# Attention's slot in a new order, and more filler in its last group: a macaron block (MoE, attention, MoE)

## The chip, the cores and the metric

The kernel runs on one core of a Trainium2 chip. The metric is device time in microseconds (us) of one execution. The core's engines are named as in the profile: PE is TensorE (PEld its weight loads), DVE is VectorE, ACT is ScalarE, POOL is GpSimd, SP is SyncE, which here only issues DMAs. Each engine works off its own queue in order.

## The reference

The input is X, 16 x 256 tokens of width 256, in float32. A feed-forward layer, an attention layer and the same feed-forward layer again are added to it:

```python
x = x + 0.5 * ffn(layernorm(x))
x = x + attn(layernorm(x))
x = x + 0.5 * ffn(layernorm(x))
```

Attention has 16 query heads and 8 key and value heads of width 32, rotary positions, a soft cap (scores are 50 tanh(scores/50)), a causal mask and softmax. The feed-forward layer normalizes its input (RMS), and returns input plus routed experts plus a shared expert:

```python
probs = softmax(x @ w_router)              # 32 experts, the best 4 of each token
g, u = buf @ w_gate[e], buf @ w_up[e]      # up to 128 tokens per expert, hidden width 176
y = (silu(g) * u) @ w_down[e]              # scattered back with the routing weight
sh = sigmoid(x @ w_shared_gate) * ((silu(x @ sw_gate) * (x @ sw_up)) @ sw_down)   # hidden width 704
return inp + out + sh
```

## The kernel before

The 4096 tokens are 32 tiles of 128, and 4 tiles make a group `g` (`NG` = 8 groups, two sequences of 256 tokens each). The residual `x` stays on chip for the whole program. There are three stages: feed-forward 0, attention, feed-forward 1.

In a feed-forward stage, each group is routed (`route`, L227: moments, transposes `pt` to `xnT`, router product `pl`, the best four, and a store of the normalized rows to the DRAM table `xtab`). Then `slots` (L310 on) gives each expert its list of tokens. The 32 experts follow (`expert`, L408): rows are gathered from `xtab` by an indirect DMA, go through gate, up and down products, and POOL scatter-adds them into the DRAM accumulator `acc`. After all experts the sums are read back (`read_sums`, L457) and added to `x`.

The shared expert depends on no expert. It is cut into pieces and used as *filler* for PE (`shared`, L371, and `Fill`, L611). For one group the pieces are: five gate chunks (`pg`, L388, eight matmuls each), one half chunk (four matmuls), and four tiles of the down product (`po`, L400, twelve matmuls each). Each piece gives a planned cost. `Fill.take(us)` adds to a balance and emits pieces until the balance is used up; overshoot is carried on, and the balance is dropped only where no group is ready:

```python
yield 1.7 * len(at)        # a gate chunk: 3.4, the half chunk 1.7
...
yield 2.6                  # one tile of the down product
```

`fill` is the shared expert of feed-forward 0, `fill2` that of feed-forward 1. A group of `fill2` is ready (`fill2.ready`) once the next routing is far enough. What is left of `fill2` after the last expert is emitted at the end by `fill2.finish(NG)`. There, groups that are done before it (`begun`) get their sums from `add_sums` on POOL; tiles that end later go through `end`, on DVE for those the last filler finishes.

Attention works by units (g, b, m): a group, one of its two sequences, and one half of the heads; 32 units in all. `scores` (L537) is a generator with two steps. Its first step makes the products of the queries with the first 128 keys into two `big` PSUM tiles `sc`, and ACT's tanh (L556) and exp (L559) and POOL's causal select (L561) on 1024 columns each; its second step does the same for the last 128 keys, with 512 columns each. `values` (L568) multiplies the probabilities by ones and by `v` into `den` and `y`, and DVE divides. `project_out` (L595) makes the output product `poa` and adds it to `x`, once per pair of units. `project` (L467) is the preparation of a group: reading the sums of feed-forward 0, adding them, moments, the normalized rows `a`, their transposes `hT`, then eight pieces of queries, keys and values (`pq`, `pv`), where rotary positions cost DVE two and POOL two instructions per `pq` piece.

A slot `k` (the loop at L742, k = 0 to 33, with j = k mod 4 and g = k // 4) puts together work of several units and groups: scores of unit k, values of unit k-1, output projection of unit k-2, projection pieces for group g+1 (`mine`) and earlier steps for g+2 (`ahead`), routing for the last stage (`routing`), and filler (`spare_time(SPARE[j])`). In the last group and the two slots behind it there is no `mine`. In this stage the order of PE, DVE, ACT and POOL is the order in which the code is written (`manual_schedule`); outside it that holds for PE, and for POOL among the experts.

PSUM is shared by three kinds of tiles, two buffers each: `big` (scores' `sc` and the filler's `pg`), `mm` (`pq`, `pv`, `pt`, `pta`, `pl`, `po`, `poa`) and `aux` (`den`, `y`).

Of the kernel before, what the change touches and what calls it, by code (L numbers as in the profile page):

```python
# [9 lines left out]
F32 = mybir.dt.float32  # L10
# [8 lines left out]
P = 128  # L19
NB, T, C = 16, 256, 256  # L20
# [25 lines left out]
MASK_FILL, ROW_FILL = 4.0, 3.2  # L46
WARM = (16, 3)
AHEAD = 3
SPARE = (1.0, 0.0, 3.0, 4.0)
PROJECT_PIECES = ((2, 1), (0, 2), (2, 1), (0, 0))  # L50

# [41 lines left out]
def macaron_kernel(ctx: ExitStack, tc: tile.TileContext, X, Wq, Wk, Wv, Wo, w_norm, w_router, w_gate, w_up,  # L93
# [314 lines left out]
    def expert(pool, n, e, idx, wd):  # L408

        xg = pool.tile([P, XW], F32, name="xg", bufs=AHEAD + 3)  # L410
        nc.gpsimd.indirect_dma_start(  # L411
# [53 lines left out]
    made = [[] for _ in range(NG)]  # L465
# [71 lines left out]
    def scores(pool, u, qT, kT):  # L537

        _, b, m = u
        t0 = b * T
        made = []
        for k0, w in ((0, T), (P, P)):
            dst = pool.tile([P, 4, 2, w], F32, name=f"p{w}", bufs=2)
            sc = [big.tile([P, 2, 2 * T], F32, tag="big", name="sc") for _ in range(2)]
            for i in range(4):
                r = slice(HD * i, HD * (i + 1))
                nc.tensor.matmul(  # L549
                    sc[i // 2][:, i % 2, 0 : 2 * w].rearrange("p (s t) -> p s t", s=2),  # L550
                    lhsT=kT[r, m, t0 + k0 : t0 + k0 + P], rhs=qT[r, m, :, t0 + T - w : t0 + T],
                    start=True, stop=True,
                )
            parts = [dst[:, 2 * h : 2 * h + 2].rearrange("p j s t -> p j (s t)") for h in range(2)]
            for h in range(2):
                nc.scalar.activation(parts[h], sc[h][:, :, 0 : 2 * w], AF.Tanh, scale=QK_SCALE / SOFTCAP)  # L556
            for h in range(2):

                nc.scalar.activation(parts[h], parts[h], AF.Exp, scale=SOFTCAP)  # L559
                diag = dst[:, 2 * h : 2 * h + 2, :, 0:P].rearrange("p j s t -> p (j s) t")  # L560
                nc.gpsimd.affine_select(  # L561
                    out=diag, in_=diag, compare_op=ALU.is_ge, fill=0.0,
                    base=0, pattern=[[0, 4], [1, P]], channel_multiplier=-1,
                )
            made.append(dst)
            yield made

    def values(pool, u, v, pa, pb, yT):  # L568


        _, b, m = u
        y = ps1.tile([P, 2, T], F32, tag="aux", name="y")
        den = ps1.tile([P, 2, T], F32, tag="aux", name="den")
        for late in range(2):
            for dst in (den, y):
                for i in range(4):
                    r = slice(HD * i, HD * (i + 1))
                    w = ones if dst is den else v[:, 2 * b + late, 4 * m + i, :]
                    if late:
                        nc.tensor.matmul(dst[r, :, P:T], lhsT=w, rhs=pb[:, i], start=False, stop=True)  # L580
                    else:
                        nc.tensor.matmul(dst[r], lhsT=w, rhs=pa[:, i], start=True, stop=False)  # L582

        dT = pool.tile([P, 2 * T // HD, HD], F32, name="dT")
        nc.vector.transpose(dT.rearrange("p n d -> p (n d)"), den.rearrange("p s t -> p (s t)"))
        rc = stat.tile([P, 2 * T // HD, 1], F32, name="rc")
        nc.vector.reciprocal(rc, dT[:, :, 0:1])
        rb = pool.tile([P, 2 * T // HD, HD], F32, name="rb")
        nc.vector.transpose(rb, rc.to_broadcast([P, 2 * T // HD, HD]))
        nc.vector.tensor_mul(  # L590
            yT[:, m].rearrange("p s t -> p (s t)"), y.rearrange("p s t -> p (s t)"),
            rb.rearrange("p n d -> p (n d)"),
        )

    def project_out(g, b, yT):  # L595
        for qh in range(2):
            t = g * GT + 2 * b + qh
            po = ps1.tile([P, C], F32, tag="mm", name="poa")
            for c in range(4):
                nc.tensor.matmul(  # L600
                    po, lhsT=yT[:, c // 2, c % 2, qh * P : (qh + 1) * P], rhs=wo[:, c // 2, c % 2, :],
                    start=(c == 0), stop=(c == 3),
                )
            nc.vector.tensor_add(x[:, t, :], po, x[:, t, :])


    def advance(work, count=1):
        for _ in range(count if work else 0):
            next(work, None)
# [32 lines left out]
    def feed_forward(n, pool, works, fill):  # L642
# [34 lines left out]

        for e in range(AHEAD):
            next(steps[e])
        with tc.manual_schedule(engines={ET.Pool}):  # L680
            for e in range(E + 2):
                if e + AHEAD < E:
                    next(steps[e + AHEAD])
                for late in range(3):
# [50 lines left out]
    units = [(g, b, m) for g in range(NG) for b in range(2) for m in range(2)]  # L735
    with tc.tile_pool(name="attn", bufs=1, reuse_waits="tile") as pool:
        probs, outs, routing = {}, {}, {}

        def spare_time(us):
            (fill if fill.done < NG else fill2).take(us)  # L740

        for k in range(len(units) + 2):  # L742
            g, j = divmod(k, 4)
            u = units[k] if k < len(units) else None
            mine, ahead = projects.get(g + 1), projects.get(g + 2)

            def unit_values():
                if 1 <= k <= len(units):
                    d = units[k - 1]
                    if d[2] == 0:  # L750
                        outs[d[:2]] = pool.tile([P, 2, 2, T], F32, name="yT")
                    values(pool, d, made[d[0]][2], *probs.pop(d), outs[d[:2]])

            if u:
                parts = scores(pool, u, *made[g][:2])
                next(parts)
            if k >= 2 and units[k - 2][2] == 1:
                d = units[k - 2][:2]  # L760
                project_out(*d, outs.pop(d))
            advance(mine, PROJECT_PIECES[j][0])
            if mine is None and j % 2 == 0:
                unit_values()
            if u:
                probs[u] = next(parts)

            if j == 0:
                advance(routing.get(g - 2))
            if j == 2:  # L770
                advance(routing.get(g - 2))
            if j == 3:
                advance(ahead)
            if mine is not None or j % 2:
                unit_values()


            if j == 3:
                advance(routing.get(g - 1))
            spare_time(SPARE[j])  # L780
            advance(mine, PROJECT_PIECES[j][1])
            if j == 1 and g >= 1:
                routing[g - 1] = route(1, g - 1)
                next(routing[g - 1])
                advance(routing.get(g - 2))
                fill2.ready = max(g - 1, 0)
            if j == 2:
                advance(routing.get(g - 1))
                advance(routing.get(g - 2))
            if j == 0:  # L790
                advance(routing.get(g - 2))

            fill.finish(min(g + 3, NG))
            if j == 3:
                advance(ahead, 2)
            elif j < 2:
                advance(ahead)
            if j == 3 and g + 3 < NG:
                projects[g + 3] = project(pp, g + 3)
                next(projects[g + 3])  # L800
        advance(routing[NG - 2], 2)
        advance(routing[NG - 1])
        fill2.ready = NG - 1
        fill2.take(LAST_FILL)
        ordered.close()
# [39 lines left out]
```

## Time and profile before

| | |
|---|---|
| median of 3 runs | 1089.79 us (1088.53 to 1090.43) |
| the profiled execution: time, and span of its instructions | 1091.85 us, 1090.1 us |
| granted TensorE clock, mean | 0.992 |
| busy share: PE, DVE, POOL, ACT | 96%, 54%, 45%, 37% |
| chain that ended last, by engine | PE 84%, DVE 8%, POOL 3%, ACT 2% |
| first scores of unit 0 begin | 395.3 us |
| last values of attention begin | 788.67 us |
| last scatter-add of an expert begins | 1057.43 us |

The profile shows one execution: the busy time of each engine, what each instruction waited for, the clock that was granted to TensorE, and the DMA traffic. In the timeline a line gives the start, the length, the engine, the source line and the operation, the tiles written and read, and how many instructions were merged. A bracket gives the idle time just before, and what ended it. In the table by windows a row gives the stretch and its length, then the busy time of PE, PEld, DVE, ACT and POOL, and last the granted clock, the DMA share and GB/s.

### The profile page before, as it was taken

What the parts mean: (1) busy time and instruction counts of PE and PEld (TensorE: products, weight loads), DVE (VectorE), ACT (ScalarE), POOL (GpSimd) and SP (SyncE); (2) the same over time, 40 slices, a digit from 0 to 9 for tenths busy, and PEclk for the clock granted to TensorE, in tenths of its full rate; (3) what the DMA queues carried; (4) which work ended last, traced back from release to release, by engine and by line L of the source; (5) the groups of instructions that cost most, each with busy time, mean ns of one, the idle gap of its engine ahead of it and who ended that gap; (6) DMA issues with size and microseconds to landing.
All of it is one profiled execution on the core that took longest, in us unless ns stands there. A gap on an engine that the chain in (4) does not pass through costs nothing.

```text
span 1090.1 us, 15694 instructions
## 1 busy us (share of the span) xinstructions
PE 1049.8 (96%) x5446; PEld 655.0 (60%) x5446; DVE 587.5 (54%) x1653; ACT 400.4 (37%) x761; POOL 492.3 (45%) x600
## 2 busy tenths in 40 slices
PE   9899999999999999989999999999999999999998
PEld 6656556777767544445455555454466467768675
DVE  5756655444453445656565657573656644444443
ACT  3333111222221256574647474745621112222211
POOL 4600102455552297777475656551411024555536
PEclk9999999999999999999999999998999999999999
DMA  8721611677773000000101010000030017777839
GB/s 268 211 96 66 202 37 37 150 168 165 171 166 57 33 21 20 1 20 2 41 1 41 2 41 1 23 17 6 23 82 22 1 33 155 161 171 155 175 60 308
DMA packets 137871, 93.00 MB, mean 85 GB/s; under 512 B 80512, under 2 KB 135104, under 8 KB 137792
## 3 DMA queue, kind: packets, MB, share of 16 engines
q1 hardware_dynamic: 125504, 74.16, 24.4%
q0 software_dynamic: 12288, 17.83, 9.4%
q8 instruction: 44, 0.72, 0.3%
q14 instruction: 35, 0.29, 0.1%
HBM read 60.99 MB, written 30.97 MB: 84 GB/s over the span
## 4 chain that ended last, share of the span: by engine, by line
PE 84%; DVE 8%; POOL 3%; ACT 2%; issue 2%; DMA 1%; SPq 0%; POOLq 0%; DVEq 0%; ACTq 0%
PE pg L388 26%; PE po L400 14%; PE pge L435 8%; PE pq L500 7%; PE poe L448 5%; PE poa L600 5%; PE sc L549 5%; PE pv L528 3%; PE den L582 2%; PE y L582 2%; PE pl L274 2%; PE pte L427 1%; DVE act L394 1%; DVE act L393 1%; DVE xr L246 1%
## 5 line engine op out<-in xcount | busy, mean ns | idle before, releaser
L388 PE MATMUL pg<-xnT,sw 128*128 128x512 f32 x704 | 320.0, 599 | 2.5 <-ACT p L556 1.8
L388 PEld LDWEIGHTS pg<-xnT,sw 128*128 128x128 f32 x704 | 130.4, 191 | 139.4 <-issue 130.4
L400 PE MATMUL po<-swd,act 128*128 128x256 f32 x768 | 182.9, 388 | 10.6 <-DVE act L394 6.4
L451 POOL DMA_INDIRECT acc<-y,idx x64 | 101.4, 1584 | 181.5 <-DMA acc<-y,idx 69.9
L400 PEld LDWEIGHTS po<-swd,act 128*128 128x128 f32 x768 | 144.8, 193 | 40.7 <-issue 12.1
L393 DVE SCALAR_TENSOR_TENSOR act<-act,pg 128x512 f32<-128x512 f32 x96 | 65.6, 684 | 172.6 <-ACT act L392 125.7
L392 ACT ACTIVATE act<-pg 128x512 f32<-128x512 f32 x96 | 57.3, 597 | 274.6 <-PE pg L388 266.8
L556 ACT ACTIVATE p<-sc 128x512 f32<-128x512 f32 (+1 forms) x128 | 97.5, 809 | 112.7 <-PE sc L549 109.1
L561 POOL TENSOR_SCALAR_AFFINE_SELECT p<-p 128x512 f32<-128x512 f32 x128 | 78.9, 640 | 84.8 <-ACT p L559 73.0
L411 POOL DMA_INDIRECT xg<-xtab,idx x64 | 67.9, 1062 | 78.8 <-DVE idx L366 59.9
L435 PE MATMUL pge<-xgT,wgu 128*112 128x128 f32 (+1 forms) x768 | 95.7, 274 | 5.8 <-issue 4.4
L559 ACT ACTIVATE p<-p 128x512 f32<-128x512 f32 (+1 forms) x128 | 100.9, 844 | 0.0
L435 PEld LDWEIGHTS pge<-xgT,wgu 128*112 128x112 f32 (+1 forms) x768 | 88.8, 182 | 8.6 <-issue 8.5
L549 PE MATMUL sc<-qT,kT 32*128 32x256 f32 (+1 forms) x512 | 68.6, 535 | 4.7 <-DVE act L394 3.4
L404 DVE SCALAR_TENSOR_TENSOR x<-po,sg,x 128x256 f32<-128x256 f32 x64 | 30.8, 482 | 78.1 <-PE po L400 74.4
L508 POOL TENSOR_TENSOR qs<-qs,kc 128x512 f32<-128x512 f32 x48 | 61.4, 1278 | 13.4 <-DVE qs L503 13.4
L394 DVE TENSOR_TENSOR act<-act,pg 128x512 f32<-128x512 f32 x96 | 65.7, 684 | 2.4
L430 ACT ACTIVATE xgT<-pte,wnorm 128x128 f32<-128x128 f32 x128 | 40.0, 365 | 71.3 <-PE pte L427 68.7
L448 PE MATMUL poe<-wd,sie 112*128 112x256 f32 x256 | 65.9, 379 | 0.1
L600 PE MATMUL poa<-wo,yT 128*128 128x256 f32 x256 | 61.5, 394 | 1.7 <-DVE qT L507 1.6
L500 PE MATMUL pq<-hT,wq 128*128 128x512 f32 x128 | 60.9, 599 | 0.0
L600 PEld LDWEIGHTS poa<-wo,yT 128*128 128x128 f32 x256 | 48.4, 194 | 20.0 <-issue 4.6
(116 smaller groups left out, 1317.7 us busy)
## 6 DMA issues: line engine op xcount, KB each, us to landing
xtab<-xr SPq DMA_DIRECT2D x16, 576.0 KB
acc<-zero SPq DMA_DIRECT2D x2, 4224.0 KB
a<-acc SPq DMA_DIRECT2D x16, 512.0 KB
wgu<-in_L_ffn_w_gate SPq DMA_DIRECT2D x64, 112.0 KB
wgu<-in_L_ffn_w_up SPq DMA_DIRECT2D x64, 112.0 KB
wd<-in_L_ffn_w_down SPq DMA_DIRECT2D x64, 112.0 KB
wgu<-in_L_ffn_w_gate SPq DMA_DIRECT2D x64, 64.0 KB
wgu<-in_L_ffn_w_up SPq DMA_DIRECT2D x64, 64.0 KB
```

Source lines behind the costliest of these rows:

```text
L388: nc.tensor.matmul(pg[:, s, :], lhsT=sw[:, c, w0 : w0 + P], rhs=xnT[:, c, cols], start=(c == 0), stop=(c == 1))
L394: nc.vector.tensor_mul(si, si, b)
L400: nc.tensor.matmul(po, lhsT=act[:, k, t * P : (t + 1) * P], rhs=swd[:, k, :], start=(k == 0), stop=(k == len(FC) - 1),)
L435: nc.tensor.matmul(pg[:fw, n_, :], lhsT=wgu[:, c, w0 : w0 + fw], rhs=xgT[:, c, :], start=(c == 0), stop=(c == 1))
L448: nc.tensor.matmul(po, lhsT=si[:, k, :], rhs=wd[:, k, :], start=(k == 0), stop=(k == 1))
L451: nc.gpsimd.indirect_dma_start(out=acc[n], out_offset=bass.IndirectOffsetOnAxis(ap=idx[:, e : e + 1], axis=0), in_=y, in_offset=None, boun ...
L500: nc.tensor.matmul(pq, lhsT=weights[:, c, :], rhs=hT[:, c, :], start=(c == 0), stop=(c == 1))
L549: nc.tensor.matmul(sc[i // 2][:, i % 2, 0 : 2 * w].rearrange("p (s t) -> p s t", s=2), lhsT=kT[r, m, t0 + k0 : t0 + k0 + P], rhs=qT[r, m, ...
L556: nc.scalar.activation(parts[h], sc[h][:, :, 0 : 2 * w], AF.Tanh, scale=QK_SCALE / SOFTCAP)
L559: nc.scalar.activation(parts[h], parts[h], AF.Exp, scale=SOFTCAP)
L561: nc.gpsimd.affine_select(out=diag, in_=diag, compare_op=ALU.is_ge, fill=0.0, base=0, pattern=[[0, 4], [1, P]], channel_multiplier=-1,)
L600: nc.tensor.matmul(po, lhsT=yT[:, c // 2, c % 2, qh * P : (qh + 1) * P], rhs=wo[:, c // 2, c % 2, :], start=(c == 0), stop=(c == 3),)
```

## The change

First scores are taken a slot earlier: those of unit k+1 are emitted in slot k. A slot now runs second scores of its unit, then values of unit k-1, then first scores of unit k+1, and only then routing, `ahead`, output projection, projection pieces and filler. The separate order for the last group (values ahead of second scores in even slots) goes. Each slot without `mine` (k = 28 to 33) asks for 3.0 more of filler. One step of the routing of group g-2 moves from the end of slot j = 2 to behind the filler of slot j = 3.

```diff
+LAST_SPARE = 3.0
 SPARE = (1.0, 0.0, 3.0, 4.0)
 PROJECT_PIECES = ((2, 1), (0, 2), (2, 1), (0, 0))
...
+        def first_scores(u):
+            parts[u] = scores(pool, u, *made[u[0]][:2])
+            next(parts[u])
+
+        parts = {}
+        first_scores(units[0])
         for k in range(len(units) + 2):
             g, j = divmod(k, 4)
             u = units[k] if k < len(units) else None
             mine, ahead = projects.get(g + 1), projects.get(g + 2)
 
-            def unit_values():
-                if 1 <= k <= len(units):
-                    d = units[k - 1]
-                    if d[2] == 0:
-                        outs[d[:2]] = pool.tile([P, 2, 2, T], F32, name="yT")
-                    values(pool, d, made[d[0]][2], *probs.pop(d), outs[d[:2]])
...
             if u:
-                parts = scores(pool, u, *made[g][:2])
-                next(parts)
+                probs[u] = next(parts[u])
+            if 1 <= k <= len(units):
+                d = units[k - 1]
+                if d[2] == 0:
+                    outs[d[:2]] = pool.tile([P, 2, 2, T], F32, name="yT")
+                values(pool, d, made[d[0]][2], *probs.pop(d), outs[d[:2]])
+            if k + 1 < len(units):
+                first_scores(units[k + 1])
+
+            if j == 0 or j == 2:
+                advance(routing.get(g - 2))
+            if j == 3:
+                advance(ahead)
             if k >= 2 and units[k - 2][2] == 1:
                 d = units[k - 2][:2]
                 project_out(*d, outs.pop(d))
             advance(mine, PROJECT_PIECES[j][0])
-            if mine is None and j % 2 == 0:
-                unit_values()
-            if u:
-                probs[u] = next(parts)
-
-            if j == 0:
-                advance(routing.get(g - 2))
-            if j == 2:
-                advance(routing.get(g - 2))
-            if j == 3:
-                advance(ahead)
-            if mine is not None or j % 2:
-                unit_values()
...
             if j == 3:
                 advance(routing.get(g - 1))
-            spare_time(SPARE[j])
+            spare_time(SPARE[j] + (0.0 if mine else LAST_SPARE))
+            if j == 3:
+                advance(routing.get(g - 2))
             advance(mine, PROJECT_PIECES[j][1])
...
             if j == 2:
                 advance(routing.get(g - 1))
-                advance(routing.get(g - 2))
```

## The prediction

> **What bounds the kernel now.** I read the page first: its totals, then its slices.
>
> ```profile
> span 1090.1 us, 15694 instructions
> PE 1049.8 (96%) x5446; PEld 655.0 (60%) x5446; DVE 587.5 (54%) x1653; ACT 400.4 (37%) x761; POOL 492.3 (45%) x600
> DMA  8721611677773000000101010000030017777839
> ```
>
> TensorE (PE) is busy 96% of the span; only some 40 us are idle. A change that removes no PE instruction can gain no more than idle time and throttled clock. In the DMA row the attention stage (slices 15 to 30) moves almost nothing, while the last slice is full. So the two ends of this change lie in places with different limits: attention on PE, the end of the program perhaps on DMA.
>
> Next the timeline of PE, attention's last group, where no projection work is left to hide waits:
>
> ```profile
> 740.30 1.13 PE L549 MATMUL sc<-qT,kT 32*128 32x512 f32 x4
> 742.50 1.65 PE L549 MATMUL sc<-qT,kT 32*128 32x512 f32 x4 [1.07 <-DVE act L394]
> ...
> 749.37 3.70 PE L388 MATMUL pg<-xnT,sw 128*128 128x512 f32 x8 [0.74 <-ACT p L556]
> ```
>
> A bracket is PE's idle time and its releaser. Both waits are for the two `big` PSUM buffers, which scores and the filler's gate products share. Six such waits from 740 to 810 us (1.07, 0.74, 0.64, 1.10, 1.07, 1.52) make 6.1 us. Then the table by windows, whose third-last number is the granted clock:
>
> ```profile
> 742.00:744.00 2.00, 1.50 (x4) 0.30 (x4) 0.45 (x1) 0.56 (x1) 0.00 (x0) 0.74 0.00 0
> 744.00:746.00 2.00, 2.00 (x14) 0.59 (x16) 0.00 (x0) 1.81 (x2) 0.00 (x0) 0.50 0.04 8
> 756.00:758.00 2.00, 2.00 (x7) 1.44 (x6) 0.00 (x0) 1.62 (x2) 0.00 (x0) 0.66 0.00 0
> 758.00:760.00 2.00, 2.00 (x7) 1.53 (x6) 0.25 (x1) 1.29 (x2) 1.27 (x2) 0.50 0.00 0
> ```
>
> Twice the clock fell to half. With 0.90 at 746 and 0.99 at 760 the lost time is 2 x (0.26 + 0.50 + 0.10 + 0.34 + 0.50 + 0.01) = 3.4 us. Last, the end of the program: the chain in order of time, then windows.
>
> ```profile
> 1056.98 18.88 PE pg L388 x44
> 1075.86 2.16 PE po L400 x10
> ```
> ```profile
> 1063.00:1065.00 2.00, 2.00 (x6) 0.80 (x6) 0.49 (x1) 0.60 (x1) 0.00 (x0) 1.00 1.00 352
> 1073.00:1075.00 2.00, 2.00 (x6) 0.92 (x5) 0.19 (x1) 0.60 (x1) 2.00 (x2) 1.00 1.09 349
> 1083.00:1085.00 2.00, 2.00 (x11) 1.77 (x10) 0.91 (x2) 0.00 (x0) 0.00 (x0) 1.00 1.08 374
> ```
>
> The last scatter-add of an expert starts at 1057.43. From there the chain is PE filler, but beside it DMA is also full (shares of 1.00 to 1.09) from 1063 to 1085: it reads 8 x 512 KB of sums and writes 4.19 MB of output. PE and DMA end within some 3 us of each other. This row decides my forecast.
>
> **The filler is moved, not removed.** `Fill.take` is a ledger: a piece costs 3.4 (gate chunk), 1.7 (half chunk) or 2.6 (a tile's down product); a group costs 5 x 3.4 + 1.7 + 4 x 2.6 = 29.1, all eight 232.8. Before, demands on `fill2` are 48 in attention, 8 LAST_FILL, then 9 + 4 + 46 + 6 + 81.6 in the last feed-forward: 202.6. Seven groups are 203.7, so one whole group is left, which is what the end of the chain shows: 44 gate matmuls, then 48 down ones. With LAST_SPARE six slots (k = 28 to 33) ask 3.0 more each. Six groups are ready then, so nothing is dropped: demand 220.6, and 12.1 is left (a half chunk and four down products). Piece by piece, slots 28 to 33 with LAST_FILL take 35.9 instead of 18.9: five more chunks. A chunk is eight matmuls of 128x512; at the end of the program the tanhs of successive chunks start at 1063.88, 1067.32 and 1070.75, a pitch of 3.43 us. That gives **+17.1 us of PE in attention**, and the PE work after the last scatter falls from 29.5 us (1056.98 to 1086.53) to 12.4.
>
> **What the last group takes up.** At most the 6.1 us idle and 3.4 us clock: 9.5. But the new order makes waits of its own. Slot 28 now runs two chunks straight before the second scores of unit 29. The second chunk's buffer comes free after ACT 0.60, DVE 0.69 and 0.69, about 2.1 us; a `pt` pair (0.6) and one score tile (0.3) cover 0.9, leaving 1.2. A chunk right behind first scores waits for their tanh (1.02 us for 1024 columns) at 0.4 to 0.5, twice; a down product behind a half chunk queues behind exp (1.06 each) at 0.6. That is about 3 us, and I leave 1 us of clock. Taken up: 5.5, bounds 0 and 9.5.
>
> **A rule that speaks against it.** The row is a half clock after single gaps of 1.07 and 0.64 us. The Trainium skill ("TensorE: Matmul & The Clock Gate", section "HAM oscillation — how this bites in real kernels") says it takes PE-idle gaps above about 3.4 us to bring the clock down; by it no wait here would cost clock, the filler could only buy idle time, and the forecast below would rise by the 2.4 us of clock I credit. The row shows the clock lost at smaller gaps, so I go by the row.
>
> **The start.** First scores of unit 0 now stand directly before its second scores. The tanh pair took 396.47 to 398.41, exp to 400.30; the second half's tanh needs 1.09 more, so first scores of unit 1 come near 401 and PE idles some 4 us where two projection pieces ran before. But unit 1 then starts 1.5 us earlier than before (402.56) and the old waits in its slot (1.11 and 0.21 at 405) go. Through the two `v` pieces I reach 415.7 where before was at 413.8: **+1.9**, bounds 0 and 4.4.
>
> **The middle, 28 slots.** Nothing is added. Before, idle PE from 412.72 to 727.73 is 2.97 + 0.20 + 0.20 + 0.54 + 1.23 = 5.1 us. In the new order second scores find tanh done a slot ago. First scores of the next unit wait for both second-half tanhs (1.09), and the values between (about 2.7) cover that; without them it would be 1.5 a slot. Moved with first scores: ACT gets 3.9 us of tanh and exp ahead of routing's copies and the projection's `a` and `hT`, and POOL gets two selects (0.64 each) ahead of the rope products (1.28 each), so those run some 3 us later in the slot. `mm` tiles behind them are held longer, but only two of them, and the queues have 30 to 40% air. Values' four DVE steps (2.5 us) now precede `x` additions; these read products that end later. Routing's last step moves behind j = 3's filler: about 3 us of small DVE work, one POOL copy (0.29), one table store on SP, read only by the experts; the next SP load of sums has a slot of slack. That takes a DVE block from ahead of `poa` additions and `pt` (old waits of 1.56 and 1.03). Against it, a chunk at j = 3 now stands closer to second scores: four times about 0.5. I take **-1**, bounds -5 (all old idle gone) and +8 (0.3 per slot, the larger of the old recurring waits).
>
> **The end.** Were it PE alone, 17 us would come back. But the last DMA byte needs 8.39 MB at 349 to 386 GB/s. Reads begin to move 5.6 us after the scatter starts and take 12 us (4.19 MB at 350); the stores 10.9 (4.19 at 386); 28.5, and 1 to 1.5 for the last landing: near 29.7, against 32.7 from 1057.43 to 1090.1 now. POOL's seven additions of sums (2.35 each from 1065.2) end at 24.3 after the scatter and keep the stores fed. So **-3.0**, bounds -4.5 and -2.
>
> **Sum:** 17.1 - 5.5 + 1.9 - 1.0 - 3.0 = +9.5. The profiled execution took 1091.85, 1.75 over its span; with the change it would be 1101.4. It stands 2.06 above the median 1089.79, so I state 1099.3, rounded to 1099. Most of the moved filler leaves a place where it hid a transfer for one where PE was already nearly full.
>
> **Rivals.** (1) *Attention hides everything* (ends on the other side): scores a slot ahead end all PSUM waits. For: the waits are real, and ACT had idle time. Price: idle from 395 to 810 (1.3 + 5.1 + 6.1) and clock 3.4 make 15.9; 17.1 - 15.9 - 4.5 = -3.3, 1086.5. It decides only if under about 1 us of wait is left in all of attention; two chunks before scores in slot 28 speak against. With 2 to 4 us left it is no measurable change (1089). (2) *The end is PE-bound*: the whole 17 come back, 17.1 - 5.5 + 1.9 - 1 - 17 = -4.5, 1085.3. That needs 8.39 MB in some 10 us, 840 GB/s; no window of the end shows over 386. Nearly excluded. (3) *A wait in every slot*: ACT or POOL falls behind because first scores hold both `big` tiles while exp, `x` and `a` stand ahead of the filler's tanh; 0.6 us in 32 slots is 19 more, about 1118. Against it: ACT is busy 0.6 of a slot. (4) *The filler isn't there*, LAST_SPARE asks and gets nothing: +1.9 - 1 and little else, 1090.7; the ledger excludes it almost.
>
> **Chances.** Forecast 0.72, its range 1094 to 1105 (the end ±1.2, the last group ±3, the middle -2 to +4); rival 1 with its weaker form 0.12; rival 2 0.02; rival 3 0.12; rival 4 0.02. For 8 in 10 I take 1091 to 1107. This kernel's runs tell 0.2% (2.2 us) from no change. Faster: rivals 1 and 2 in part, 0.07; within: 0.09; slower: 0.84.
>
> **What would show it.** Right: 4 gate and 48 down matmuls left after the last scatter; PE idle over 10 us there while DMA shares stay near 1.09 and the chain ends on POOL or a store; the last scatter some 12 us later than 1057.4; five more `pg` groups from 740 to 825; no more than 4 us idle there. Wrong: the distance from last scatter to end falls well below 28 us (the end was PE's), or attention's end moves by under 5 us (the waits were worth more), or a bracketed wait on `sc` or `pg` repeats in every slot (rival 3).

## The result, and the profile after

The changed kernel takes 1127.3 us (median of 6 runs, 1123.05 to 1133.68) against 1090.18 of the kernel before beside it: 1.0339 times as long, with a 95% interval of 1.0302 to 1.0377. The forecast of 1099 had the sign; the loss of 37 us is four times the 9 us forecast, and lies outside the range. The profiled execution took 1133.68 us. All line numbers of the changed kernel and its variants are one higher than before, since `LAST_SPARE` is a new line.

The page of the changed kernel shows as many matmuls as before and 2.3 us more PE work (1049.8 before), in a span 42 us longer:

```profile
span 1132.0 us, 15674 instructions
PE 1052.1 (93%) x5446; PEld 656.5 (58%) x5446; DVE 593.4 (52%) x1653; ACT 399.3 (35%) x761; POOL 492.5 (44%) x597
```

So nearly all of it is time in which PE has no matmul running. Three places in the two traces split it. Attention's last filler ends at 844.84 instead of 809.73: +35.1. The last scatter-add begins at 1101.87 instead of 1057.43: +44.4. From there to the end of the span it is 30.1 us instead of 32.7: -2.6. The end behaved as forecast (-3.0), and so did the ledger: 4 gate and 48 down matmuls were left. Attention did not.

The stretch between, from attention's last filler to the last scatter-add, is 9.3 us longer (257.0 against 247.7). The profile is of the slowest of the six runs, 6.4 us above their median; the later profiles with the filler have 3.5 us (two `yT` buffers) and 2.0 (the old order) there. What lengthened this stretch was not settled.

PE's waits in attention, by who ended them, the first three of the changed kernel (us in total, times, longest):

```profile
PE pt L256 <- DVE x L605: 11.1, 7, 4.4
PE pv L529 <- DVE x L605: 6.7, 6, 1.1
PE sc L550 <- ACT p L557: 4.7, 5, 1.8
```

The first was small before, and the second is new:

```profile
PE pt L255 <- DVE x L604: 1.4, 2, 1.0
```

In both PE waits for an `mm` tile that DVE has yet to empty, by adding an output product `poa` to `x`. DVE's timeline in slot 5 (a slot j = 1) shows why it is late, and PE's timeline what it holds up:

```profile
452.80 0.71 DVE L590 STREAM_TRANSPOSE rb<-rc 128x512 f32<-128x512 f32 x1
456.80 0.69 DVE L591 TENSOR_TENSOR yT<-y,rb 128x512 f32<-128x512 f32 x1 [3.29 <-PE poa L601]
457.41 0.74 DVE L605 TENSOR_TENSOR x<-poa,x 128x256 f32<-128x256 f32 x2
```
```profile
453.04 3.72 PE L601 MATMUL poa<-wo,yT 128*128 128x256 f32 x16
457.88 3.72 PE L529 MATMUL pv<-wv,hT 128*128 128x256 f32 x16 [1.11 <-DVE x L605]
```

DVE is done with `rb` at 453.5 and then stands idle 3.29 us until PE has finished `poa`. The `yT` that it wants to write has a single buffer, and `poa` is still reading it: the values of an even unit open a new pair and write a new `yT`, and in the new order they stand ahead of the output projection of the old pair. Before, that projection came first. Both additions to `x` are queued behind the waiting write, both `mm` tiles stay full until then, and the next product on PE loses 1.11 us. Over the stage DVE waits so in 14 slots:

```profile
DVE yT L591 <- PE poa L601: 35.8, 14, 3.4
```

Measured from values to values, the slots of groups 3 and 4 show the same in each odd slot (us):

| slot | 12 | 13 | 14 | 15 | 16 | 17 | 18 | 19 |
|---|---|---|---|---|---|---|---|---|
| before | 10.4 | 13.4 | 13.9 | 14.3 | 10.4 | 13.4 | 14.6 | 12.9 |
| after | 10.3 | 14.6 | 13.7 | 15.5 | 10.3 | 14.6 | 14.4 | 13.7 |
| after, two `yT` buffers | 10.3 | 13.2 | 13.7 | 14.1 | 10.3 | 13.2 | 14.4 | 12.7 |

### The profile page after: what moved, and what is told of

Read it like the earlier page. It is cut to its first block, busy times and chain, and to the rows that moved or that the text cites. A ratio compares the mean times of both kernels' runs of the same rounds, so it can differ in the third digit from the quotient of the medians.

```text
span 1132.0 us, 15674 instructions
## 1 busy us (share of the span) xinstructions
PE 1052.1 (93%) x5446; PEld 656.5 (58%) x5446; DVE 593.4 (52%) x1653; ACT 399.3 (35%) x761; POOL 492.5 (44%) x597
## 4 chain that ended last, share of the span: by engine, by line
PE 82%; DVE 8%; POOL 2%; ACT 2%; DMA 2%; issue 2%; SPq 1%; DVEq 0%; POOLq 0%; ACTq 0%
PE pg L389 24%; PE po L401 14%; PE pge L436 8%; PE pq L501 7%; PE poe L449 5%; PE sc L550 5%; PE poa L601 5%; PE den L583 3%; PE pv L529 3%; PE y L583 2%; PE pl L275 2%; PE pte L428 1%; PE den L581 1%; DMA a<-acc 1%; PE y L581 1%
## 5 line engine op out<-in xcount | busy, mean ns | idle before, releaser
L297 POOL COPY xr<-pr 128x128 f32<-128x128 f32 x16 | 4.8, 299 | 130.4 <-DVE pr L296 87.4
```

## The experiments

**A second yT buffer, and the parts of the change alone.** The room for a second buffer was made by writing `rb` into `dT`, which DVE has read by then:

```diff
-    outs[d[:2]] = pool.tile([P, 2, 2, T], F32, name="yT")
+    outs[d[:2]] = pool.tile([P, 2, 2, T], F32, name="yT", bufs=2)
...
-        rb = pool.tile([P, 2 * T // HD, HD], F32, name="rb")
+        rb = dT
```

> The changed kernel with two yT buffers instead of one (to make room, rb is written into dT, which DVE has read by then). Theory A, single yT: the values of an even unit now stand ahead of the output projection that still reads the old yT, DVE waits at L591 for PE poa, the x additions queue behind it, and PE's next mm tile waits 1.1 us in 13 odd slots and 4.4 us once, with clock lost behind it. Then the brackets from DVE x vanish, about 19 us of idle and some 3 of clock come back: near 1105 from 1127.3. Theory B, first scores ahead of all other work delay ACT and POOL and with them the mm tiles: a second yT does little, the time stays above 1120.

The changed kernel without the filler:

```diff
-LAST_SPARE = 3.0
+LAST_SPARE = 0.0
```

> The changed kernel with LAST_SPARE 0: the new order alone. By the forecast's terms the filler costs 17.1 less what the last group takes up (0 to 9.5) less 3.0 at the end: 5 to 14 us, so 1113 to 1122. If the end were PE-bound the filler would cost nothing, and the time would not fall below 1125.

The kernel before with nothing but the filler:

```diff
+LAST_SPARE = 3.0
...
-            spare_time(SPARE[j])
+            spare_time(SPARE[j] + (0.0 if mine else LAST_SPARE))
```

> The kernel before with only the extra filler (LAST_SPARE 3.0 in the slots without projection work), old order. By the forecast's terms 17.1 - 5.5 - 3.0 = +8.6 (+5 to +14): about 1099. If the end were PE-bound: 1084 to 1090. If the order is the larger part, this takes less than a third of the 37 us.

Both edits to the changed kernel, so that the order is alone and without its wait:

> The changed kernel with two yT buffers and LAST_SPARE 0: the order alone without the wait for yT. Theory A with the forecast's terms: +1.9 at the start, -1 in the middle, the last group as before, so 1088 to 1096. Theory B: the order costs by itself, above 1105.

| kernel | median us | ratio to before (95%) |
|---|---|---|
| two `yT` | 1108.85 | 1.0175 (1.0155 to 1.0194) |
| `LAST_SPARE` 0 | 1111.04 | 1.0209 (1.0182 to 1.0236) |
| before with the filler | 1103.87 | 1.0128 (1.0106 to 1.0150) |
| two `yT`, `LAST_SPARE` 0 | 1094.64 | 1.0049 (1.0032 to 1.0066) |

The kernel before took 1089.13 beside them. The second buffer gives back 18.5 us with the filler (1127.3 to 1108.85, each measured at another time) and 16.4 without (1111.04 to 1094.64). Theory A holds, and the profile with the buffer has no wait of DVE to write `yT`. The edit also puts `rb` into `dT`, but both are read by DVE alone, so no other engine holds them up. Only two waits of PE for an addition to `x` are left:

```profile
PE pt L256 <- DVE x L605: 5.2, 2, 4.4
```

The filler costs 14.7 us in the old order and 14.2 in the new one with two buffers: more than the 8.6 of the forecast, a little over the upper bound I had set. In the changed kernel itself it costs 16.3, which puts `LAST_SPARE` 0 some 2 us below the range I gave. The order without its wait costs 5.5. The three, 16.4 + 14.2 + 5.5, make 36.1 of the 37.1. (The 5.5 was expected as -1 to +7 in total, and the time lies in that range.)

**Does the end's DMA keep the filler from paying back?** At the end of "before with the filler" PE is done at 1083.4 and idle for over 19 us, with DMA full (the stretch and its length, busy us and instructions of PE, PEld, DVE, ACT and POOL, PE's granted clock, DMA share, GB/s):

```profile
1078.00:1085.00 7.00, 5.44 (x26) 4.45 (x24) 1.45 (x3) 0.00 (x0) 4.25 (x2) 1.00 1.04 343
1085.00:1095.00 10.00, 0.00 (x0) 0.00 (x0) 3.75 (x3) 0.00 (x0) 10.00 (x6) 0.63 1.09 365
```

Two kernels take most of that DMA away, without and with the filler. They read and add the sums only for groups 6 and 7 and store the other six without them, so they leave out a part of the computation:

```diff
-            for g in range(NG):
-                sums[g] = read_sums(sp, 1, g, NG)
+            for g in range(NG - 2, NG):
+                sums[g] = read_sums(sp, 1, g, 2)
             for g in range(begun):
-                add_sums(g, sums[g])
+                if g in sums:
+                    add_sums(g, sums[g])
```

> The kernel before with less DMA at the end: the sums of the last feed-forward are read and added for the last two groups only, the other six groups are stored without them (that part of the computation is left out). The chain at the end is then PE filler alone, as it was: 1087 to 1091, no change to speak of.

> The same shortened end with LAST_SPARE 3.0 in the old order (with the whole end: 1103.87, 14.7 above before). If the end's DMA was what kept the moved filler from paying back, the end now follows PE: about 15 us after the last scatter instead of 30, and the time is within 3 us of the run with the shortened end alone, 1086 to 1092. If the filler costs by itself in attention, whatever the end does, it stays near 1100 to 1104.

Measured: 1089.46 without the filler (ratio to before 1.0008, 0.9990 to 1.0026) and 1089.84 with it (0.9994, 0.9976 to 1.0013). With the short end the filler costs 0.4 us; with the whole end it cost 14.7. The distance from the last scatter-add to the end of the span is 17.4 us (1069.12 to 1086.5) with filler and short end, 30.5 with filler and whole end. So the filler's price is what the end does not let come back. The two kernels also spare POOL six of its additions of sums. In the whole end with filler those are done at 1097.3, while the DMA share is between 0.92 and 1.10 in every 2 us from 1078 to 1100; so the transfers set the length of the end, as that trace reads.

**The start.** In "two `yT`, `LAST_SPARE` 0" PE's timeline begins so:

```profile
397.51 0.70 PE L550 MATMUL sc<-qT,kT 32*128 32x256 f32 x4 [1.11 <-ACT p L557]
398.42 0.70 PE L550 MATMUL sc<-qT,kT 32*128 32x256 f32 x4 [0.21 <-ACT p L557]
400.89 2.47 PE L550 MATMUL sc<-qT,kT 32*128 32x512 f32 x8 [1.77 <-ACT p L557]
```

The last line takes 2.47 us where 1.14 is usual: the granted clock (third number from the end) was 0.77 from 400 to 402 and 0.50 from 402 to 404.

```profile
400.00:402.00 2.00, 1.11 (x6) 0.89 (x8) 0.00 (x0) 2.00 (x5) 0.85 (x3) 0.77 0.00 0
402.00:404.00 2.00, 2.00 (x7) 0.50 (x2) 0.00 (x0) 1.42 (x3) 1.04 (x2) 0.50 0.00 0
```

The next kernel puts the two projection pieces of slot 0 between its first and second scores:

```diff
+            if k == 0:
+                advance(mine, PROJECT_PIECES[j][0])
             if u:
                 probs[u] = next(parts[u])
...
-            advance(mine, PROJECT_PIECES[j][0])
+            advance(mine, PROJECT_PIECES[j][0] if k else 0)
```

> Two yT buffers and LAST_SPARE 0 (measured 1094.64), and in slot 0 alone the two projection pieces go between the first and the second scores of unit 0. Theory: what is left of the order's cost (5.5 us) is mostly the start, where PE waits 1.11 + 0.21 + 1.77 us and the clock then falls: 2.5 to 4 us come back, 1090.5 to 1092. Rival: the cost is spread over the middle (POOL and ACT later in every slot): above 1093.5.

Measured: 1089.92, ratio 1.0010 (0.9995 to 1.0025). That is 4.7 us back, more than the 2.5 to 4 expected, and 0.6 below the range of times I gave; the rival falls.

**A cure by order instead of a buffer.** In the changed kernel the output projection goes ahead of the values:

```diff
             if u:
                 probs[u] = next(parts[u])
+            if k >= 2 and units[k - 2][2] == 1:
+                d = units[k - 2][:2]
+                project_out(*d, outs.pop(d))
             if 1 <= k <= len(units):
...
-            if k >= 2 and units[k - 2][2] == 1:
-                d = units[k - 2][:2]
-                project_out(*d, outs.pop(d))
```

> The changed kernel, one yT buffer and LAST_SPARE 3.0 as changed; only the output projection is moved ahead of the values in the slot, as it stood before. Theory A (DVE waits for the poa that reads the old yT): this cures the same wait without a second buffer, so the time is that of the kernel with two yT buffers, 1105 to 1112 (measured there 1108.85), and the 1.1 us brackets from DVE x are gone. If the second buffer had helped by something else (another layout of memory, rb in dT), the time stays above 1118.

Measured: 1140.65, ratio 1.0475 (1.0441 to 1.0510). The expectation missed by 30 us. DVE's wait to write `yT` and PE's waits for additions to `x` are gone, as theory A says, but the kernel is slower than the changed one. Its slot 15 (j = 3), PE and then ACT:

```profile
603.27 3.70 PE L389 MATMUL pg<-xnT,sw 128*128 128x512 f32 x8 [0.59 <-ACT p L557]
606.81 0.68 PE L492 MATMUL pta<-kc,a 128*128 128x128 f32 x4
608.75 0.66 PE L492 MATMUL pta<-kc,a 128*128 128x128 f32 x4 [1.26 <-ACT xnT L259]
609.33 0.70 PE L550 MATMUL sc<-qT,kT 32*128 32x256 f32 x4
610.68 0.70 PE L550 MATMUL sc<-qT,kT 32*128 32x256 f32 x4 [0.65 <-DVE act L395]
611.31 1.80 PE L583 MATMUL den<-p,ones 128*32 128x512 f32 x8
```
```profile
602.19 1.94 ACT L557 ACTIVATE p<-sc 128x1024 f32<-128x1024 f32 x2 [5.79 <-PE sc L550]
604.02 2.00 ACT L560 ACTIVATE p<-p 128x1024 f32<-128x1024 f32 x2
605.91 2.07 ACT L482 ACTIVATE a<-x,hb,s 128x256 f32<-128x256 f32 x4
607.87 0.82 ACT L259 ACTIVATE xnT<-pt,wnorm 128x256 f32<-128x256 f32 x2
```

ACT runs without a break from 602.19 to the end of these lines, 6.5 us, on the first scores and on `a` and `xnT` behind them. PE needs each of these within the slot, and the 3.7 us of `poa` that stood between first scores and them now lies ahead. Three waits follow (0.59, 1.26, 0.65), and then values at a lower clock (0.50 from 612 to 614): 1.80 us instead of 1.06. Over the stage PE's waits for `a` and `xnT` have grown; in the changed kernel they were 1.2 and 0.3 us:

```profile
PE pta L492 <- ACT a L482: 9.6, 3, 4.5
PE pta L492 <- ACT xnT L259: 4.8, 4, 1.3
```

To see whether it is these slots, the next kernel moves the projection in slots j = 1 only:

```diff
+            if j != 3 and k >= 2 and units[k - 2][2] == 1:
+                d = units[k - 2][:2]
+                project_out(*d, outs.pop(d))
             if 1 <= k <= len(units):
...
-            if k >= 2 and units[k - 2][2] == 1:
+            if j == 3 and units[k - 2][2] == 1:
```

> The changed kernel (one yT, LAST_SPARE 3.0) with the output projection ahead of the values in slots j = 1 only; in slots j = 3 it stays behind first scores. Moving it in both gave 1140.65 although the yT wait was gone. Theory: in slots j = 3 the output products behind first scores cover ACT's run of tanh, exp, a and xnT; taken away there, PE waits for ACT and the clock falls. Then this kernel keeps that cover, and pays the yT wait (1.4 us a slot) in eight slots j = 3 only: 1112 to 1121. If the loss came from slots j = 1 or from both alike: above 1125.

Measured: 1122.28 (1118.94 to 1126.22), ratio 1.0294 (1.0264 to 1.0323): a gain of 18.4 over moving it in both, and 1.3 above the range I gave. The j = 3 slots cause most of that loss; something is left in j = 1 too. PE's waits for `a` and `xnT` are back to 1.2 and 0.5 us. So what I had as rival 3, ACT behind first scores, is real, but `poa` covers it in the change as it was made.

**One slot of the middle.** With the start mended, one slot is still 4.8 us longer than before (slot 7, 15.76 against 10.95 from values to values). DVE and then PE, around it:

```profile
468.46 0.73 DVE L504 STREAM_SHUFFLE qs<-pq 128x512 f32<-128x512 f32 x1
469.09 0.67 DVE L508 TENSOR_TENSOR qT<-pq,kc 128x512 f32<-128x512 f32 x1
469.68 4.76 DVE L247 TENSOR_SCALAR xr<-x,mv,s 128x256 f32<-128x256 f32 x4
```
```profile
477.28 0.66 PE L256 MATMUL pt<-kc,xr 128*128 128x128 f32 x4 [4.45 <-DVE x L605]
```

Ahead of these lines DVE had waited 4.53 us for a `qs` buffer, that is for POOL's rope products, which now queue behind two selects of first scores; then four `xr` steps took 4.76 beside POOL. In the kernel before, these were 2.94 and 4.02, and the additions to `x` came straight after `xr`; now the four steps of values (2.4 us) stand between, and PE waits 4.45. In group 1 there is no filler yet to hide this. The edit moves `xr` of that slot into the wait:

```diff
             spare_time(SPARE[j] + (0.0 if mine else LAST_SPARE))
...
+            if j == 2 and g == 1:
+                advance(routing.get(g - 1))
             advance(mine, PROJECT_PIECES[j][1])
...
-            if j == 2:
+            if j == 2 and g != 1:
                 advance(routing.get(g - 1))
```

> Two yT buffers, LAST_SPARE 0, the start mended (measured 1089.92), and in group 1, slot j = 2, the four xr steps of the routing ahead of the third projection piece. There DVE sat idle 4.5 us for POOL and then ran xr for 4.7, and PE waited 4.4 for an x addition behind it. Theory: that one slot (15.8 us against 10.9 before) is what is left; 3 to 5 us come back, 1085 to 1087, below the kernel before. Rival: the third mm tile is then held longer and PE waits for it instead: no change, 1089 to 1091.

Measured: 1084.01 (1083.36 to 1087.85), ratio **0.9949 (0.9930 to 0.9968)**: faster than the kernel before by 0.3 to 0.7%, and 1 us below the range I gave. Slot 7 takes 11.7 us. With its one buffer, its first slot and this one mended, and the filler where it was, the kernel with the new order thus gains some 6 us. Whether an earlier `xr` would help the old order too, no run shows.

**The moved step alone**, in the kernel before:

```diff
             spare_time(SPARE[j])
+            if j == 3:
+                advance(routing.get(g - 2))
             advance(mine, PROJECT_PIECES[j][1])
...
                 advance(routing.get(g - 1))
-                advance(routing.get(g - 2))
```

> The kernel before with one part of the change alone: the step of the routing of group g-2 moved from the end of slot j = 2 to behind the filler of slot j = 3. The forecast put it into the -1 of the middle: 1087 to 1090, no change that can be told. A gain of 2 us or more would say that its DVE block had made the old waits for x additions and pq tiles; a loss, that POOL's wait for pr now stands before the selects.

Measured: 1089.49, ratio 0.9993 (0.9981 to 1.0005): nothing that can be told, as expected.

## Why the prediction was wrong, by its own steps

- *The middle, -1 with bounds -5 and +8.* This is the step that failed. The sentence "Values' four DVE steps (2.5 us) now precede `x` additions; these read products that end later" counted the time of those four steps and not what the last of them writes. `yT` has one buffer, and the moved output projection is its reader. Measured: 16.4 us. The prediction did say what is queued behind the values on DVE; it did not ask whether the values themselves would now wait. The rest of the middle came out as hoped: with two buffers slots 12 to 19 are 0.1 to 0.2 us shorter than before. Slot 7 was 4.8 longer. That is of the kind that the prediction described for POOL ("so those run some 3 us later in the slot") and for the values' steps ahead of the additions, and priced at nothing.
- *The last group takes up 5.5.* Mis-sized. In the old order with the filler, the stretch from first scores of unit 28 (740.18) to the end of LAST_FILL's pieces (822.85) is 82.7 us against 69.4: of 17.1 moved, 3.8 were taken up. Four of the six waits stayed (3.55 of 6.1 us). They end when ACT or DVE frees one of the two `big` tiles that `pg` and scores share, and here more work of the same kind did not change that. (The sixth, the 1.52, was of `po` for an `mm` tile; the prediction read it as one more for `big`.) Three of the four:

```profile
742.38 1.55 PE L550 MATMUL sc<-qT,kT 32*128 32x512 f32 x4 [1.07 <-DVE act L395]
...
749.25 7.13 PE L389 MATMUL pg<-xnT,sw 128*128 128x512 f32 x16 [0.74 <-ACT p L557]
...
758.52 1.13 PE L550 MATMUL sc<-qT,kT 32*128 32x512 f32 x4 [0.64 <-DVE act L395]
```

  These are waits of before, in the same sizes, with the filler added behind them. Another 2.0 us were lost between LAST_FILL and the last scatter-add (249.7 against 247.7); their cause was not settled. With the end's -2.2 this makes 13.1 us in the two profiles, and 14.7 in the medians, against 8.6 forecast.
- *The start, +1.9.* Mis-sized, within its bounds. With two buffers and no filler PE is done with the two `v` pieces at 417.36, where the prediction had 415.7 and the kernel before 413.8: +3.6. PE idled 3.1 us for some 4 forecast, but I priced that at full clock. The mend gave 4.7 us.
- *The end, -3.0.* Right: -2.6 in the changed kernel, -2.2 in the old order with filler, and that the end holds the filler's time back is shown by the two kernels with a short end. Rival 2 is refuted by the same pair.
- *A wait in every slot (rival 3, 19 us, 0.12).* It came nearest in price, through another mechanism: a buffer, in odd slots only. Its own mechanism appeared where `poa` was moved away.
- *The clock.* I held the trace's row against the page on the clock. Again no single gap of PE reached the 3.4 us of the Trainium skill ("TensorE: Matmul & The Clock Gate", section "HAM oscillation — how this bites in real kernels"): at the start the gaps were 1.11, 0.21 and 1.77, PE was idle 3.1 of 4.5 us, and the clock was 0.50 just after. The measurement decides: here the clock fell without a single gap that long. That the filler would raise the clock, as I had credited, was not borne out either: in the old order with filler both dips of the last group came again (0.50 from 744 to 746 and 0.51 from 760 to 762).

## To carry to other kernels

When a step is moved ahead of another on an in-order engine, list what it writes as well as what it computes: if the step it overtakes still reads that buffer, the moved one waits for it and so does all that is queued behind. Filler that hides a transfer is not free to be moved, even into a place with idle time; the idle time must come from a lack of work, not from the order around a buffer. And a product behind a long run on another engine may be its cover: see what it hides before giving it a new place.

## What the runs showed of the hardware

DVE's four `xr` steps (128x256 each) took 1.38 us with POOL idle, 2.33 beside POOL's selects and 4.76 beside its rope products. The Trainium skill ("SBUF — State Buffer", section "SBUF: two separate sides") describes a port pair that GpSimd and some of VectorE's instructions share by an exclusive lock, where the loser waits out the other's whole instruction. The three durations agree with it (1.19 us a step beside rope products of 1.28, 0.58 beside selects of about 0.6), though no run here isolates the lock.

The spread of the changed kernel (1123.05 to 1133.68) goes with its granted clock: 0.985 in the two fastest runs, 0.982 in the next two, 0.978 and 0.977 in the two slowest. Why the clock differs between executions, no run shows. PE at half clock at the end (0.50 from 1115 us on in the profiled run) costs nothing, since it has no work there.
